# Offset convolution: summing columns of taps on VectorE before shifting them on TensorE

## The chip, the cores and the metric

One core of one Trainium2 chip. The metric is the device time of one execution in microseconds (us), a median of several. The profile is one execution of each kernel; PE is TensorE's matmuls, PEld its weight loads, DVE VectorE, ACT ScalarE, POOL GpSimd, and SPq the queue from which SyncE (SP) issues transfers.

## The reference, cut to what matters

Two layers on an image batch of shape (2, 256, 128, 128) in fp32. The first holds three deformable branches with dilations 1, 9 and 12. Each needs its sampling offsets first: 18 numbers per pixel, from a 3x3 convolution of the normalised image.

```python
def _branch(x, w_off, w_def, lw, lb, pad, dil):
    off = _conv(x, w_off, pad, dil)            # 18 channels out, 3x3, dilated: the part changed
    y = _deform_dw(x, off, w_def, pad, dil)    # bilinear sampling at the offsets
    return gelu(_ln2d(y, lw, lb))
x1 = _branch(x, off_w1, def_w1, bw1, bb1, 1, 1)
x2 = _branch(x, off_w2, def_w2, bw2, bb2, 9, 9)
x3 = _branch(x, off_w3, def_w3, bw3, bb3, 12, 12)
# ... a 1x1 convolution, norms and an MLP, then a second layer: group norm and a ternary 3x3 convolution
```

## The kernel before

It runs in three stages: the offsets and, from them, "hat" functions (the bilinear weights, stored to memory); the sampling; the final convolution. The change is in the first stage, which does image 0 and then image 1. Per row, TensorE multiplies 128 pixels by all 27 x 18 tap weights and the result goes into a ring of 40 rows (`zr`). Then, for 8 rows at a time (a group, `G`; 16 groups per image), each of the 27 taps is taken from the ring with its row offset and shifted along the image by a product with a 0/1 matrix.

```python
def columns(g):                                   # 4 rows of the image: a column step
    xt = pool.tile([P, KC, R, W], F32, name="xa", tag="xa", bufs=4)
    nc.scalar.dma_start(xt, x[b]...)              # the image's load, ScalarE's queue
    # ... normalise, transpose, store the rows to `table` (SyncE's queue)
    for r in range(R):
        # pz = xt[row r] @ wz, two products
        (nc.scalar.copy if r % 2 else nc.vector.tensor_copy)(zr[:, (g * R + r) % ZRING, :], pz[:, 0:NZ])

def offsets(G):
    todo = []                                     # (branch, tap, shift, row, ring slot, rows)
    for br, dil in enumerate(DILS):
        for tap in (4, 0, 1, 2, 3, 5, 6, 7, 8):
            # ... cut where the ring wraps, or where the image ends
    for i, (br, tap, dx, r0, s, n) in enumerate(todo):
        z0 = (br * 9 + tap) * 18
        nc.tensor.matmul(pov[:, r0:r0+n, br*18:br*18+18], lhsT=k["shift"][:, dx, :],
                         rhs=zr[:, s:s+n, z0:z0+18], start=i == 0, stop=i == len(todo) - 1)
    # offs <- po; offs is stored (SyncE) and split into bf16 parts

def make_hats(g, parts, r0):                      # twice per group
    # ... transposes of the parts (pp), then six blocks:
    for h0 in range(0, 9 * NH, HCH):
        # ph = two products; hb = |ph| by ScalarE (bufs=8); hb = min(hb, 1) - 1 by VectorE
        # store_hats: 4 or 6 stores of 18 to 144 KB per block, all nc.sync.dma_start
```

All stores and the 1 MB loads for the normalisation's statistics (`xt`) leave through SyncE's one queue, in program order. A group of 8 rows is 56 hat stores, two table stores and one offset store: 59 issues.

## Time and profile before

8689.66 us median of 3 runs (8687.26 to 8691.22).

| what | before |
|---|---|
| span of the profiled run | 8672.1 us |
| first stage, to the last hat store | 0 to 1281 us |
| PE busy over the span, DVE busy | 90%, 69% |
| records of offset products (two per fp32 product) | 1872 |
| mean granted TensorE clock | 0.952 |

Read it by stages. The first stage is only 15% of the time; a share of the whole span says nothing about it. The prediction shows the lines. The lines are as the profile gives them.

### The profile page before, as it was taken

The page shows a single profiled execution, that of the slowest core. Times are in us where ns is not written, and L with a number is a line of the kernel's source. Part 1 is how long each engine was busy: PE and PEld are TensorE (multiplying, and loading weights), DVE is VectorE, ACT ScalarE, POOL GpSimd, SP SyncE. Part 2 cuts the span into 40 slices and gives each one's busy share as a digit, 9 for nine tenths or more (in the row PEclk, how much of TensorE's full clock was granted, in tenths as well). Part 3 has the DMA queues.
Part 4 walks back from the last instruction along what each step waited for, and adds up shares of the span by engine and source line. Part 5 has one row for each costly group of instructions (what it writes and reads, how often), then busy time and mean ns, then how long its engine had stood idle before and what let it go on. Part 6 is the DMA issues. An engine that isn't in the chain of part 4 may idle for free. (4 is left out here: it accounts for less than half of the span.)

```text
span 8672.1 us, 125470 instructions
## 1 busy us (share of the span) xinstructions
PE 7799.2 (90%) x41584; PEld 5835.1 (67%) x41584; DVE 5965.6 (69%) x13113; ACT 4513.1 (52%) x9542; POOL 718.1 (8%) x1292
## 2 busy tenths in 40 slices
PE   6977967898999999999979999989999979999999
PEld 3644637777787778777777787777877744444444
DVE  5434436889898998987688989898988843222222
ACT  1332324566666666666656666666666752221221
POOL 0000000011111111111101111111111110000000
PEclk9988978999999999999999999999999989999999
DMA  7445448999999999987799899999898821111111
GB/s 239 138 144 165 139 138 224 245 243 241 248 241 248 243 245 244 242 240 218 190 244 244 244 244 243 245 243 248 239 247 238 237 99 56 57 56 54 58 57 41
DMA packets 994675, 1661.78 MB, mean 192 GB/s; under 512 B 139424, under 2 KB 540112, under 8 KB 989656
## 3 DMA queue, kind: packets, MB, share of 16 engines
q1 hardware_dynamic: 976600, 1620.03, 68.3%
q10 hardware_dynamic: 17408, 33.56, 1.3%
q8 instruction: 333, 5.46, 0.3%
q14 instruction: 334, 2.74, 0.1%
HBM read 1385.08 MB, written 268.09 MB: 191 GB/s over the span
## 5 line engine op out<-in xcount | busy, mean ns | idle before, releaser
L766 PE MATMUL pm<-A,xs 128*128 128x180 f32 (+2 forms) x22288 | 3661.4, 321 | 569.6 <-ACT ev L775 530.9
L766 PEld LDWEIGHTS pm<-A,xs 128*128 128x128 f32 x22288 | 3456.9, 197 | 776.5 <-ACT ev L775 630.8
L775 ACT COPY ev<-pm 128x360 f32<-128x360 f32 (+2 forms) x5572 | 2285.6, 455 | 1528.6 <-DVE ring L740 749.8
L740 DVE SCALAR_TENSOR_TENSOR ring<-ev,defw,ring 128x256 f32<-128x256 f32 (+5 forms) x6272 | 2787.3, 464 | 211.3 <-ACT ev L775 42.0
L1078 PE MATMUL pc<-cring,signs 128*128 128x512 bf16 x6912 | 1503.5, 380 | 4.1 <-ACT cring L1059 3.4
L696 DVE TENSOR_TENSOR A<-hy,hx 128x768 f32<-128x768 f32 x1130 | 1017.9, 947 | 343.2 <-DMA hx<-hats 177.8
L1078 PEld LDWEIGHTS <-signs 128*128 128x128 bf16 x6912 | 671.8, 97 | 835.4 <-issue 8.4
L481 ACT ACTIVATE T<-T,rs 128x256 f32<-128x256 f32 x1280 | 663.6, 595 | 4.0 <-POOL rs L477 3.9
L1090 DVE SCALAR_TENSOR_TENSOR o<-pc,wpn,o 128x512 f32<-128x512 f32 x128 | 96.1, 751 | 675.1 <-PE pc L1078 675.0
L474 POOL TENSOR_SCALAR rs<-mv 128x4 f32<-128x4 f32 x320 | 113.0, 353 | 5150.6 <-DVE mv L472 4290.9
L440 PE MATMUL hp<-T,w 128*128 128x512 f32 x1024 | 489.0, 602 | 7.8 <-ACT T L559 7.8
L1086 ACT ACTIVATE o<-xl,l1b 128x512 f32<-128x512 f32 x128 | 92.2, 722 | 739.4 <-DMA out_x<-o 715.7
L207 PE MATMUL pz<-wz,xa 128*128 128x486 f32 x1024 | 469.2, 583 | 6.6 <-DVE zr L214 3.5
L470 DVE BATCH_NORM_STATS2 st<-T 128x6 f32<-128x256 f32 x1280 | 447.4, 413 | 22.5 <-ACT T L462 22.4
L440 PE MATMUL h<-hT,w 128*128 128x512 f32 x1024 | 460.1, 592 | 0.0
L1059 ACT CAST cring<-rest 128x768 bf16<-128x768 f32 (+1 forms) x256 | 211.8, 828 | 462.7 <-PE pc L1078 296.9
L493 PEld LDWEIGHTS zc<-ident,T 128*128 128x128 f32 x2560 | 339.6, 155 | 98.7 <-issue 61.4
L287 ACT ACTIVATE hb<-ph 108x512 f32<-108x512 f32 x384 | 222.6, 598 | 338.8 <-DMA hats<-hb 229.8
L509 ACT ACTIVATE T<-zc,bb,bw 128x512 f32<-128x512 f32 x384 | 278.6, 780 | 227.6 <-PE zc L493 226.9
L493 PE MATMUL zc<-ident,T 128*128 128x128 f32 x2560 | 379.2, 294 | 19.2 <-ACT T L481 13.8
L476 POOL TENSOR_TENSOR rs<-rs,mhalf 128x4 f32<-128x4 f32 x320 | 368.5, 1152 | 0.0
L462 ACT COPY T<-tp 128x512 f32<-128x512 f32 x640 | 344.2, 597 | 36.4 <-PE tp L460 35.3
(107 smaller groups left out, 5381.2 us busy)
## 6 DMA issues: line engine op xcount, KB each, us to landing
hy<-hats SPq DMA_DIRECT2D x1114, 384.0 KB
hx<-hats SPq DMA_DIRECT2D x1114, 384.0 KB
xs<-table SPq DMA_DIRECT2D x1876, 128.0 KB
g12d<-T SPq DMA_DIRECT2D x128, 512.0 KB
other<-g12d SPq DMA_DIRECT2D x128, 512.0 KB
xl<-x1d SPq DMA_DIRECT2D x120, 384.0 KB
hats<-hb SPq DMA_DIRECT2D x256, 144.0 KB
xa<-in_x ACTq DMA_DIRECT2D x64, 512.0 KB
```

Source lines behind the costliest of these rows:

```text
L207: nc.tensor.matmul(pz[:, 0:NZ], lhsT=xt[:, c, r, :], rhs=k["wz"][:, c, :], start=c == 0, stop=c == KC - 1,)
L440: nc.tensor.matmul(out, lhsT=w, rhs=v, start=i == 0, stop=i == n - 1)
L462: nc.scalar.copy(Tv[:, 2 * h : 2 * h + 2, :].rearrange("p j c -> p (j c)"), tp)
L470: pin(nc.vector.bn_stats(st[:, j, :], Tv[:, j, :]))
L476: nc.gpsimd.tensor_tensor(rs[:, 0, :], rs[:, 0, :], mhalf[:, 0:NB4], ALU.pow)
L481: nc.scalar.activation(Tv[:, j, :], Tv[:, j, :], AF.Identity, scale=rs[:, 0, j : j + 1], bias=rs[:, 1, j : j + 1],)
L493: nc.tensor.transpose(zc[:, j * P : (j + 1) * P], Tv[:, j, c * P : (c + 1) * P], ident)
L696: nc.vector.tensor_tensor(dst, hy[:, :, i0 * W : i1 * W].rearrange("p t (i w) -> p t i w", w=W), hx[:, :, i0 * W : i1 * W].rearrange("p t ...
L740: nc.vector.scalar_tensor_tensor(dst, src, w, dst, ALU.mult, ALU.add)
L766: nc.tensor.matmul(pm[:, j, 0:n], lhsT=xts[b, Rt][T + j][:, c * P : (c + 1) * P], rhs=A[:, m0:m1, AO + (T + j) * CI : AO + (T + j + 1) * C ...
L775: nc.scalar.copy(ev[:, m0:m1, T * CI : (T + 2) * CI].rearrange("p m (t j) -> p t m j", j=CI), pm[:, :, 0:n].rearrange("p t (m j) -> p t m ...
L1078: nc.tensor.matmul(pc, lhsT=signs[:, k, ky * 3 + kx, m * P : (m + 1) * P], rhs=xc[:, i, k, ky : ky + R, kx : kx + W], start=j == 0, stop=j ...
```

## The change

Shifting along the image (x) is the same for the three taps of a column (same kx, three ky). So VectorE first adds the three rows of the ring that belong to one output row, for all three kx at once, and TensorE shifts the sums: 9 products per group, with no cuts, in place of 27 and more.

```diff
+            zs = pool.tile([P, 3, ZG, 3 * 18], F32, name="zs", tag="zs", bufs=2)
             for br, dil in enumerate(DILS):
-                for tap in (4, 0, 1, 2, 3, 5, 6, 7, 8):
-                    ...
+                for y, n, mid in rows(0, y0, y1):
+                    for ya, na, up in rows(-1, y, y + n):
+                        nc.vector.tensor_tensor(zs[...], mid[...], up, ALU.add)
+                    # ... plain copies where a row has no neighbour above
+                for y, n, down in rows(1, y0, y1):
+                    nc.vector.tensor_tensor(dst, dst, down, ALU.add)
-            for i, (br, tap, dx, r0, s, n) in enumerate(todo):
-                nc.tensor.matmul(... rhs=zr[:, s : s + n, z0 : z0 + 18] ...)
+            for br, dil in enumerate(DILS):
+                for kx in range(3):
+                    nc.tensor.matmul(
+                        pov[:, :, br * 18 : br * 18 + 18],
+                        lhsT=k["shift"][:, k["dxs"].index((kx - 1) * dil), :],
+                        rhs=zs[:, br, :, kx * 18 : kx * 18 + 18],
+                        start=br == 0 and kx == 0, stop=br == 2 and kx == 2)
```

(cut: the boundaries of the image and of the ring)

More of the change, by code (lines that the diff above doesn't have):

```diff
@@ L221, in offsets, with rows @@
             pov = po[:, 0 : ZG * NOFF].rearrange("p (r n) -> p r n", n=NOFF)
-            todo = []
+            zs = pool.tile([P, 3, ZG, 3 * 18], F32, name="zs", tag="zs", bufs=2)
             for br, dil in enumerate(DILS):
-                for tap in (4, 0, 1, 2, 3, 5, 6, 7, 8):
-                    ky, kx = tap // 3 - 1, tap % 3 - 1
-                    y = max(G * ZG, -ky * dil)
-                    y1 = min((G + 1) * ZG, H - ky * dil)
+                def rows(ky, y, y1):
+                    y, y1 = max(y, -ky * dil), min(y1, H - ky * dil)
                     while y < y1:
@@ L230, in offsets @@
                         n = min(y1 - y, ZRING - s)
-                        todo.append((br, tap, k["dxs"].index(kx * dil), y - G * ZG, s, n))
+                        z0 = (br * 3 + ky + 1) * 54
+                        yield y, n, zr[:, s : s + n, z0 : z0 + 54]
                         y += n
-            for i, (br, tap, dx, r0, s, n) in enumerate(todo):
-                z0 = (br * 9 + tap) * 18
-                nc.tensor.matmul(
-                    pov[:, r0 : r0 + n, br * 18 : br * 18 + 18],
-                    lhsT=k["shift"][:, dx, :],
-                    rhs=zr[:, s : s + n, z0 : z0 + 18],
-                    start=i == 0,
-                    stop=i == len(todo) - 1,
-                )
+                y0, y1 = G * ZG, (G + 1) * ZG
+                for y, n, mid in rows(0, y0, y1):
+                    done = y
+                    for ya, na, up in rows(-1, y, y + n):
+                        if ya > done:
+                            nc.vector.tensor_copy(
+                                zs[:, br, done - y0 : ya - y0], mid[:, done - y : ya - y]
+                            )
+                        nc.vector.tensor_tensor(
+                            zs[:, br, ya - y0 : ya - y0 + na], mid[:, ya - y : ya - y + na], up,
+                            ALU.add,
+                        )
+                        done = ya + na
+                    if done < y + n:
+                        nc.vector.tensor_copy(
+                            zs[:, br, done - y0 : y + n - y0], mid[:, done - y : n]
+                        )
+                for y, n, down in rows(1, y0, y1):
+                    dst = zs[:, br, y - y0 : y - y0 + n]
+                    nc.vector.tensor_tensor(dst, dst, down, ALU.add)
[5 more added lines that the diff above has]
+                        rhs=zs[:, br, :, kx * 18 : kx * 18 + 18],
+                        start=br == 0 and kx == 0,
+                        stop=br == 2 and kx == 2,
+                    )
             offs = pool.tile([P, ZG, NOFF], F32, name="offs", tag="offs", bufs=2)
```

## The prediction

> **What bounds the kernel now.** I read the page's slices first, because a change in one stage is worth only what that stage can give back. The span of 8672.1 us has three stages. The offset convolution lives in the first one, which ends at about 1281 us (slices 1 to 6 of 216.8 us each); then come the sampling (to about 7100 us) and the final convolution.
>
> ```profile
> PE   6977967898999999999979999989999979999999
> DVE  5434436889898998987688989898988843222222
> ...
> PEclk9988978999999999999999999999999989999999
> ```
>
> The first stage handles the two images one after the other, and each time TensorE (PE) is nearly full and then falls away. So I cut the stage at the points where the last row of column products has been copied out (573 us for image 0, 1148 us for image 1) and at the ends of the images' stores:
>
> ```profile
> core 0: us, PE busy (x) PEld busy (x) DVE busy (x) ACT busy (x) POOL busy (x), PEclk, DMA share, GB/s
> 139.00:573.00 434.00, 417.76 (x2014) 268.48 (x2013) 181.99 (x399) 139.55 (x256) 0.00 (x0) 0.97 0.50 144
> 573.00:675.00 102.00, 47.98 (x147) 23.42 (x146) 23.43 (x57) 24.36 (x41) 0.00 (x0) 0.55 0.44 125
> 752.00:1148.00 396.00, 390.58 (x1879) 249.06 (x1878) 164.66 (x363) 126.65 (x233) 0.00 (x0) 1.00 0.49 141
> 1148.00:1281.00 133.00, 74.99 (x294) 42.55 (x292) 36.44 (x88) 37.51 (x65) 0.65 (x1) 0.61 0.45 127
> ```
>
> Two regimes per image: a body of 434 and 396 us with PE busy 96 and 99% and VectorE (DVE) only 42%, and a tail of 102 and 133 us in which no engine is half full. The waits of PE in the body of image 1 confirm that nothing holds it there: 5.4 us in all.
>
> ```profile
> PE ph L279 <- ACT hb L287: 3.6, 4, 1.1
> PE pz L207 <- DVE xa L154: 1.1, 2, 0.7
> PE tpa L193 <- ACT ts L198: 0.7, 3, 0.2
> ```
>
> In the tail I looked for what is full, and it is the queue of SyncE (SP), which issues the small stores of the hat functions one by one:
>
> ```profile
> 656.96 0.36 SPq L308 DMA_DIRECT2D hats<-hb  x1
> 657.37 0.49 SPq L304 DMA_DIRECT2D hats<-hb  x1
> 657.90 0.37 SPq L308 DMA_DIRECT2D hats<-hb  x1
> 658.37 0.34 SPq L304 DMA_DIRECT2D hats<-hb  x1
> 658.75 0.38 SPq L308 DMA_DIRECT2D hats<-hb  x1
> 659.17 0.78 SPq L304 DMA_DIRECT2D hats<-hb  x2
> ```
>
> Each start follows the one before by about 0.42 us. Counted over 600 to 675 us there are 169 issues in 75 us, 0.444 us each. An image has 16 groups of 8 rows, each with 56 such stores, and 48 other stores: 944 issues, some 415 us at that rate. So SP is a second, hidden limit close behind PE: in the body it is occupied only 71% (635 issues at 0.427 us in 380 us), in the tail it sets the pace at 26 to 28 us a group. Last, what the offset products cost:
>
> ```profile
> L235 PE MATMUL po<-zr,shift 128*128 128x144 f32 x606 | 84.9, 287 | 0.0
> L207 PE MATMUL pz<-wz,xa 128*128 128x486 f32 x429 | 195.9, 576 | 1.1 <-DVE xa L154 1.1
> L260 DVE TENSOR_TENSOR rest<-offs,parts 128x432 f32<-128x432 f32 x13 | 7.9, 606 | 0.3
> 305.32 3.39 PE L235 MATMUL po<-zr,shift 128*128 128x18 f32 x28
> 308.99 2.29 PE L235 MATMUL po<-zr,shift 128*128 128x72 f32 x18
> ```
>
> The mean of 287 ns is a latency; the matmuls overlap. The runs give the real price: 3.39 us for 28, 2.29 us for 18, and over all runs of 4 or more in the body 113.6 us for 856, 0.133 us a record.
>
> **What the Trainium skill says.** "TensorE: Matmul & The Clock Gate", Back-to-back issue gap: the spacing of a stream of weight loads and matmuls is set by both together, about 81 ns at 128 columns. The trace agrees in kind, not in size: fp32 offset records come 0.121 to 0.136 us apart, nearly whatever their width (the slivers left by the ring's wrap cost as much as whole blocks), so the count of products is what counts. "VectorE: DVE Perf Modes", The TRN2 errata: an fp32 tensor_tensor takes (N+151)/0.96 ns; for N=432 that is 607 ns, and the trace has 606 to 607 ns for L260. "Perfetto Trace Analysis", DMA Instruction — HWDGE: a DMA instruction's time in the profile is the issuing sequencer's and the descriptor generator's, not the movement of the data. That fits: stores of 18 and 36 KB all take about 0.37 us of SP while the DMA share is 0.44. The same page, Optimization Strategy: the most contended engine can change between regimes; here it does, twice per image.
>
> **The change part by part.** Removed: the trace has 1872 records of offset products; the program has 936, so an fp32 product is two records. After the change there are 9 per group, 288 products, 576 records. That is 1296 fewer, times 0.133 = 172 us of PE, 86 us per image. Not all lies on the path. In the bodies of the built order the changed program still has about 252 records per image, against 858 and 786 in the trace, so about 606 and 534 go: 80 and 71 us. Before the first group's first store another 18 products (36 records) per image go: 5 us each, most of it given back below. What is left falls in the tails, where PE idles half of the time and nothing is gained.
>
> Added: the built program has 226 additions and copies for the column sums, where the ring does not wrap six additions of 432 elements per group. At 607 ns for a full one, and N/0.96 plus the fixed 157 ns for the cut ones, they come to 118 us of DVE, 3.7 us per group. DVE goes from about 13.6 us of 33 per group (42%) to 17.3 of some 28.5 (61%): it does not become the bound. They lie beside PE's work, except that the first products of a group now wait for an eviction and one addition (0.66 + 0.61 us) where no other column's work stands between; in the order of PE the nine products of a group are mostly surrounded by others. For the first group of each image nothing stands in between: 1 to 3 us back.
>
> Moved: in the SP order the stores stay in their sequence of 56 per group, two table stores and one of the offsets between. PE's order still ends the columns with twelve groups of hats done and four to go. So the tail stays: four groups at SP's pace, 102 and 133 us.
>
> PE per group now, from the pitches: 32 column records at 0.405 us (13 us), 24 hat records at 0.295 (7.1), 16 plane transposes at 0.165 (2.7), 16 table transposes at 0.13 (2.1), 58.5 offset records at 0.133 (7.8): 32.7 us, and the traced spacing of the stores' groups is 34.5 us in image 0 and 33.8 us in image 1. After: 18 offset records, 2.4 us, sum 27.3 us. SP needs 59 issues at 0.44, 26 us. Two stages in tandem with 27.3 and 26 us and only eight hat buffers between them (two thirds of a group's twelve), and with only two buffers for the table's rows, which leave through the same SP queue: I choose 29 us a group, 1.7 us of stalls over PE's own need (the traced spacing now exceeds PE's need by 1.1 to 1.8 us, while SP has 29% to spare). Gain of the bodies: 12 x (34.5 - 29) + 12 x (33.8 - 29) = 66 + 58 = 124 us. The starts give about nothing net, the tails, the sampling and the end nothing. 8690 - 124 = 8566, rounded to 8565 us.
>
> **The rivals.** (1) PE's saving comes through whole: SP keeps up without stalls. Gain 80 + 71 + a few, about 155 us, 8535 us. For it: PE's order spreads the hat products evenly, and SP's 26 us are below 27.3. Against it: SP's queue is in order and arrives in bursts of 56, and the hats already waited for stores in the body of image 1 (ACT 50.8 us in 33 waits), when SP was far from full. (2) SP takes over as the bound and PE stalls behind it: 31 us a group, gain 76 us, 8614 us. For it: just those waits; a late store holds ACT, then DVE behind its hb steps, then the additions queued behind those, and then the products. Against it: the offsets of a group are made two groups before its hats are stored, so the additions have slack. (3) The additions make DVE late: each group pays 1 to 3 us where PE waits for the last sum, gain 60 to 100 us. DVE at 61% in program order speaks for some of it. (4) Nothing gained, since the stores end the stage anyway. Against: SP was idle for 29% of the body because PE fed it no faster, so an earlier hat is an earlier store.
>
> **Range and chances.** 8565 us, 8525 to 8620 us. The low end is rival 1 and a little more, the high end rival 2. Faster by over 2% means under about 8516 us, a gain of 174 us, as much as all PE time removed, tails included: 0.06. Slower by over 2% would need 174 us lost in a stage where nothing grows but an engine at 61%: 0.01. Within 2%: 0.93.
>
> **What would show it.** Right: 576 offset records of about 0.13 us pitch; some 226 new VectorE instructions of 118 us in all; the groups of stores 28 to 30 us apart in the bodies; SP occupied over 80% there; tails still some 100 to 130 us at the 0.50 clock; the stage ends near 1157 us and the later stages take as long as before. PE waits for hb and DMA grow in the body. It would be wrong if the groups came at 33 us still (the additions are on the path, shown by PE waiting at the offset products), if the tails grew by what the bodies lost (SP the only bound), or if the later stages changed because buffers or order moved there.

## The result, and the profile after

The changed kernel takes 8624.71 us (8612.09 to 8632.42, 4 runs) against 8688.46 us of the kernel before on the same chip (8682.11 to 8691.22): 64 us less, where 124 were predicted, and 5 us above the stated range. The ratio is 0.9926, with a 95% interval of 0.9909 to 0.9943; a ratio here is the mean time of one kernel's runs over that of the other's runs of the same rounds, so it isn't quite the quotient of the medians. Executions over 1.5% slower than the fastest of the same kernel are left out of the means. The result is correct.

First the parts that I had counted. Offset products and additions in the profile of the changed kernel, grouped by shape; the columns are count, then busy us and mean ns of one:

```profile
L258 PE MATMUL po<-zs,shift 128*128 128x144 f32 x576 | 90.0, 295 | 19.4 <-DVE offs L266 19.4
L244 DVE TENSOR_TENSOR zs<-zr 128x432 f32<-128x432 f32 x72 | 40.9, 601 | 11.0 <-ACT zr L214 11.0
L255 DVE TENSOR_TENSOR zs<-zs,zr 128x432 f32<-128x432 f32 x68 | 40.0, 600 | 32.1 <-ACT zr L214 31.9
```

576 records, as computed, and 0.6 us for a full addition. The durations of all 226 new VectorE instructions sum to 117 us. So the counts of what was removed and added are as predicted; what it was worth is not.

The two images again, with the right cuts: from about the first hat store to the last copy into the ring (the body), and from there to the last hat store (the tail). Busy us of each engine in each stretch, kernel before:

```profile
145.00:534.00 389.00, 382.45 (x1850) 245.43 (x1850) 165.74 (x364) 124.64 (x230) 0.00 (x0) 1.00 0.49 142
535.00:675.00 140.00, 76.71 (x292) 43.64 (x291) 36.91 (x86) 37.45 (x65) 0.00 (x0) 0.60 0.47 133
757.00:1149.00 392.00, 386.25 (x1860) 246.84 (x1860) 161.86 (x357) 125.74 (x232) 0.00 (x0) 1.00 0.49 141
1149.00:1281.00 132.00, 74.32 (x292) 42.43 (x291) 36.44 (x88) 37.22 (x65) 0.65 (x1) 0.61 0.44 126
```

and the changed kernel:

```profile
131.00:495.00 364.00, 335.93 (x1292) 182.61 (x1290) 207.50 (x460) 124.53 (x230) 0.00 (x0) 0.96 0.54 152
495.00:636.00 141.00, 73.36 (x230) 35.82 (x229) 40.10 (x93) 38.33 (x66) 0.00 (x0) 0.56 0.49 138
723.00:1082.00 359.00, 330.51 (x1291) 181.57 (x1289) 200.34 (x447) 125.18 (x230) 0.00 (x0) 0.97 0.53 150
1082.00:1222.00 140.00, 69.46 (x231) 33.34 (x230) 39.61 (x95) 38.38 (x66) 0.65 (x1) 0.59 0.47 130
```

The bodies shrink from 389 to 364 and from 392 to 359 us. PE was 98% busy in them and is now 92%, at a granted clock that falls from 1.00 to 0.96 and 0.97: TensorE is still the fullest engine, but something now holds it up. How much of the loss is the lower clock, no run isolates. DVE rises from 42% to 56 and 57% and is far from full. The sum of the whole stage, from the exact starts of the stores: first store 14.4 us earlier, bodies 25.6 and 32.1 us shorter, tails 1.1 and 7.2 us longer, the stretch between the images 4 us longer: 60 us. The later stages differ by 2 us.

What PE waits for in the body of image 1 (us in total, times, longest), changed kernel; before it was 5.4 us in three rows:

```profile
PE ph L302 <- ACT hb L310: 9.0, 16, 1.6
PE pz L207 <- DVE xa L154: 7.1, 5, 2.0
PE po L258 <- DVE offs L266: 6.1, 4, 2.4
PE tpa L193 <- ACT ts L198: 5.6, 9, 2.0
PE pp L294 <- DVE parts L284: 0.5, 1, 0.5
```

28.3 us, from four different sides, and hardly any of it at the sums `zs`. I read waits scattered like this as back pressure from further on: the hat blocks (`hb`), the offsets (`offs`) and the table rows (`ts`) are all buffers that come free when a store has landed. So I took SyncE's queue apart. Over the first 11 groups of 56 hat stores, counted from single records (a line of the timeline can merge several stores and hide a wait between them):

| body | us per group | SP issuing | gaps under 0.15 us | longer waits of SP |
|---|---|---|---|---|
| before, image 0 / 1 | 35.1 / 35.3 | 24.1 / 23.9 | 3.2 / 3.2 | 7.7 / 8.1 |
| after, image 0 / 1 | 33.0 / 32.8 | 23.8 / 23.7 | 3.2 / 3.2 | 6.0 / 5.9 |

The queue's own work is 27 us a group, the same in both kernels, and equal to what TensorE needs after the change (27.3 us by the prediction). What the change took away is about 2 us a group of SP's waiting, and 6 us of waiting stayed. A stretch of that queue in the changed kernel (start us, us):

```profile
302.75 0.94 SPq L199 DMA_DIRECT2D table<-ts  x2
303.74 0.79 SPq L275 DMA_DIRECT2D offd<-offs  x1
304.62 1.31 SPq L331 DMA_DIRECT2D hats<-hb  x1
305.99 0.83 SPq L327 DMA_DIRECT2D hats<-hb  x1
306.87 0.73 SPq L331 DMA_DIRECT2D hats<-hb  x1
307.65 0.78 SPq L327 DMA_DIRECT2D hats<-hb  x2
308.47 0.36 SPq L331 DMA_DIRECT2D hats<-hb  x1
310.17 0.29 SPq L327 DMA_DIRECT2D hats<-hb  x1
```

Most hat stores take 0.36 to 0.39 us as before, but the three that follow the table's and the offsets' stores take 1.31, 0.83 and 0.73 us, and between 308.83 and 310.17 us the queue waits.

### The profile page after: what moved, and what is told of

The parts are those of the page before. It is cut to its first block, busy times and chain, and to the rows that moved or that the text cites.

```text
span 8610.4 us, 123172 instructions
## 1 busy us (share of the span) xinstructions
PE 7669.1 (89%) x40288; PEld 5674.0 (66%) x40288; DVE 6061.3 (70%) x13339; ACT 4516.2 (52%) x9542; POOL 718.7 (8%) x1292
```

## The experiments

Two theories at first. A: the path of the hat stores through SyncE's queue sets the pace. B: VectorE is late because of the additions. C was a variant: VectorE held up by the offsets' buffers. Chips differ by some 10 us, so each run is told against the kernel before on the same chip; the change alone gained 64 us by that measure. The interval of a gain is about 14 us to each side, so two gains that differ by less than some 20 us are not told apart. The last column is the time from an image's first hat store to its last, divided by 16 groups, in the profiled run.

| run | us | before, same chip | gain | ratio, 95% interval | us per group, image 0 / 1 |
|---|---|---|---|---|---|
| before | | 8688 | | | 33.1 / 32.7 |
| the change | 8625 | 8688 | 64 | 0.9909 to 0.9943 | 31.6 / 31.2 |
| e1 no additions | 8632 | 8681 | 49 | 0.9932 to 0.9966 | 31.8 / 31.3 |
| e2 changed, two queues | 8382 | 8681 | 298 | 0.9639 to 0.9672 | 25.8 / 25.3 |
| e3 before, two queues | 8505 | 8681 | 176 | 0.9784 to 0.9817 | 28.4 / 28.1 |
| e4 four offset buffers | 8636 | 8681 | 44 | 0.9938 to 0.9971 | 32.0 / 31.6 |
| e5 ten hat buffers | 8633 | 8677 | 44 | 0.9934 to 0.9967 | 31.6 / 31.4 |
| e6 other stores moved | 8558 | 8677 | 119 | 0.9853 to 0.9886 | 29.7 / 29.1 |
| e7 one block in six | 8623 | 8677 | 55 | 0.9918 to 0.9951 | 31.9 / 30.2 |
| e8 no additions, two queues | 8389 | 8677 | 288 | 0.9658 to 0.9695 | 26.0 / 25.7 |
| e9 changed, loads moved | 8590 | 8677 | 88 | 0.9890 to 0.9923 | 30.5 / 30.5 |
| e10 before, loads moved | 8656 | 8677 | 21 | 0.9962 to 0.9995 | 32.4 / 32.7 |
| e11 one in six and loads | 8584 | 8679 | 95 | 0.9876 to 0.9909 | 30.8 / 30.7 |
| e12 hats alone on SP | 8553 | 8679 | 126 | 0.9841 to 0.9874 | 29.0 / 29.1 |
| e13 one block in three | 8461 | 8676 | 215 | 0.9733 to 0.9765 | 27.2 / 26.2 |
| e14 statistics loads moved | 8578 | 8676 | 98 | 0.9876 to 0.9909 | images overlap, see there |

**e1: no additions.** Wrong result; the additions and `zs` are gone, the rest is the changed kernel.

```diff
-                        rhs=zs[:, br, :, kx * 18 : kx * 18 + 18],
+                        rhs=zr[:, G*ZG % ZRING : G*ZG % ZRING + ZG, (br*3+1)*54 + kx*18 : (br*3+1)*54 + kx*18 + 18],
```

> A wrong result on purpose: the nine products per group read the middle row of the column products directly, with no additions by VectorE; everything else is the changed kernel. Theory A (the hat stores in SyncE's one queue, with the few buffers behind them, set the pace of about 31 us a group): within 15 us of the changed kernel's 8625, groups still 30 to 32 us apart in the bodies. Theory B (VectorE in program order is late because of the 118 us of additions): down by 60 to 100 us to about 8525 to 8565, groups 27 to 28 us apart. Theory C (VectorE is held by the offsets' two buffers, whose stores stand behind the hat stores in the queue): little change, 0 to 20 us.

8631.6 us, a gain of 49 us in place of 64, groups at 31.8 and 31.3 us. With 117 us of VectorE's work removed, nothing is gained. Theory B falls.

**e2 and e3: two queues.** Every second of the six hat blocks is stored from GpSimd's queue, in the changed kernel (e2) and in the kernel before (e3).

```diff
-                    store_hats(g, q, h, hb[p : p + m])
+                    store_hats(g, q, h, hb[p : p + m], nc.gpsimd if h0 // HCH % 2 else nc.sync)
```

> The changed kernel with every second block of hats stored from GpSimd's queue instead of SyncE's. Theory A: groups at PE's own need, 27 to 28 us in the bodies, and tails of about 60 us in place of about 140: down by some 150 us to 8450 to 8500. Theory B: the tails shorten but the bodies stay at 31 us: 8540 to 8580. Theory C: between them, since the offsets' stores stand behind half as many others.

> The kernel before with the same two queues. Theory A: TensorE still sets about 33 us a group in its bodies, only the tails shorten: 8590 to 8630, so that the change is worth 110 to 150 us once the stores are out of the way, against 64 with one queue. Theory B: the difference between the two kernels stays about 64 us.

8382.47 and 8505.27 us, both correct, both better than expected. The change, which was worth 64 us with one queue, is worth 123 us here, which happens to be near what I had predicted. The bodies of e2, same columns as above:

```profile
137.00:497.00 360.00, 339.90 (x1402) 191.06 (x1401) 247.22 (x535) 145.59 (x269) 212.56 (x371) 0.99 0.79 220
577.00:933.00 356.00, 338.72 (x1408) 190.86 (x1408) 223.37 (x491) 145.85 (x271) 216.56 (x377) 1.00 0.66 182
```

As long as in the changed kernel, but with 13.5 groups of hats stored in each in place of 11.0, so a group takes 26 to 27 us in the body, about TensorE's own need. The tails fall from 140 to about 50 us. And image 1's first copy into the ring comes at 524 us, while the hats of image 0 are stored until 549; with one queue its statistics loads stand behind those stores, and that copy came at 677 us. In the built program the loads stand between the groups of image 0 now. So e2 changes two things besides the queues: the start of image 1, which e13 and e14 take apart, and the order of TensorE's work, which no run isolates: see the end of the next section.

**e4: four buffers for the offsets.**

```diff
-            offs = pool.tile([P, ZG, NOFF], F32, name="offs", tag="offs", bufs=2)
+            offs = pool.tile([P, ZG, NOFF], F32, name="offs", tag="offs", bufs=4)
-        hatw = ap.tile([P, 2, 9 * NH], F32, name="hatw32")
+        hatw = k["zr"]...[:, 0 : 18 * NH]          # staged in the ring, to make room
```

> The changed kernel with four buffers for the offsets in place of two (room made by staging the hat matrix in the ring). Theory C: VectorE's 65 us of waits for the offsets' store go and 30 to 60 us of time with them, 8565 to 8595. Theory A: VectorE waits elsewhere instead, within 15 us of 8625. Theory B: within 15 us.

8636.45 us, no gain over the change. Removing VectorE's waits for the offsets' store does not help; theory C falls too.

**e5: ten hat buffers** (`bufs=8` to `bufs=10` at `hb`, with the same room made).

> The changed kernel with ten buffers for the blocks of hats in place of eight (the hat matrix staged in the ring, as in the run with four offset buffers, to make room). Theory A1 (the number of instructions that SyncE's queue has to issue sets the pace; deeper buffers only lengthen the queue): within 15 us of 8625 to 8636. Theory A2 (the eight buffers, each held until its stores have landed, set the pace): a quarter more of them takes 40 us or more off, 8590 or less.

8632.85 us, no gain over the change: two more hat buffers do not help either.

**e6: the table's and the offsets' stores from GpSimd's queue.**

```diff
-            nc.sync.dma_start(tv[2 * REACH + g * R : ...], ts)
+            nc.gpsimd.dma_start(tv[2 * REACH + g * R : ...], ts)
-            nc.sync.dma_start(offd[b][G * ZG : ...], offs)
+            nc.gpsimd.dma_start(offd[b][G * ZG : ...], offs)
```

> The changed kernel with the table's and the offsets' stores (3 of the 59 issues of a group) on GpSimd's queue, all hats still on SyncE's. Theory A1: 56 instead of 59 issues, 30 us instead of 31.5 us a group: 20 to 50 us less, 8575 to 8605. Theory A3 (the order in one queue binds: a table or offset store at its head waits, and the hats behind it with it): the waits of SyncE in the body, 4 to 5 us a group, go with them, 8520 or less.

8557.9 us: 55 us more gained than by the change alone. That is between the two expectations: more than three issues in 59 explain, less than all of SP's waits. SP's longer waits in the body did not fall (7.4 and 6.9 us a group), but TensorE's waits there fell from 28 to 7 and 6 us, so its columns end at 459 us. Fewer groups are stored by then: the tails, 5 groups of 28 us after the change alone, are 6 groups of 25 us here.

**e7: one block in six from GpSimd's queue** (`nc.gpsimd if h0 // HCH == 2`).

> The changed kernel with one of the six blocks of hats of each half group stored from GpSimd's queue: SyncE issues 51 instead of 59 per group. Theory A1: the spacing falls with the count, 31.5 x 51 / 59 = 27.2 us, which is TensorE's own need, and the tails by an eighth: some 100 to 120 us less, 8505 to 8525. Theory A2 or A3: the buffers, or the stores at the head of the queue, still bind: 8570 to 8610.

8622.59 us: no gain over the change, though SP issues 51 times per group in place of 59. Its issuing falls to 21 us a group in the body, and its longer waits rise to 10.5 and 9.3. So the count of issues alone isn't the cause; this was my clearest miss among the experiments.

**e8: no additions, two queues** (e1 and e2 together, wrong result).

> A wrong result on purpose: two queues as in the best run so far (8382 us), and no additions by VectorE. If the additions lie beside TensorE's work even where TensorE sets the pace: within 15 us of 8382. If they delay the products once the stores no longer bind: 30 to 60 us less, 8320 to 8350.

8389.37 us, no faster than e2. The additions lie beside TensorE's work even where TensorE sets the pace.

**e9 and e10: the image's loads from GpSimd's queue**, in the changed kernel and in the kernel before. In the built program the stores of SyncE and these loads of ScalarE take turns in eight completion semaphores, and the profile puts most of SP's waits down to them. In the body of image 1, before:

```profile
SPq L304 <- DMA xa<-in_x: 54.1, 11, 9.2
SPq L308 <- DMA xa<-in_x: 21.4, 10, 6.9
```

and after the change:

```profile
SPq L327 <- DMA xa<-in_x: 25.0, 12, 6.4
SPq L331 <- DMA xa<-in_x: 22.1, 11, 5.4
```

```diff
-            nc.scalar.dma_start(xt, x[b]...)
+            nc.gpsimd.dma_start(xt, x[b]...)
```

> The changed kernel with the image's loads (64 in all, 512 KB each) issued from GpSimd's queue instead of ScalarE's; all 59 stores of a group stay on SyncE. In the built program the stores and these loads share eight completion semaphores in turn, so that a hat store waits for the load that had its semaphore before, and a load for a store. Theory L (this tie is what holds the stores back: the waits of SyncE for the image's loads, 53 us in the first image): those waits vanish, groups at 27 to 28 us, 60 to 160 us less than the changed kernel's 8625, 8465 to 8565. Theory A1 (the plain issue rate of 59 stores): at most 20 us less, 8605 or more.

> The kernel before with the same loads moved to GpSimd's queue. Theory L: TensorE still needs 32.7 us a group, the stores keep up, only the tails and the last groups of the bodies gain: 20 to 70 us below 8680, 8610 to 8660, so that the change is worth 100 us or more in this pair. Theory A1: within 15 us of 8680, and the change is worth about 60 us again.

8589.85 and 8656.06 us. The waits for the loads are gone, but most of SP's longer waits stay (4.5 and 5.1 us a group in e9, 6.0 and 5.9 before): the profile now puts them down to hat blocks that aren't made yet and to other stores. Both kernels gain about the same, 24 us and 21 us, and the change is worth 66 us in this pair. The tie costs some 20 us; it isn't what took the change's gain.

**e11 and e12: combinations.** e7 with e9; and e6 with e9, so that only hats are left to SP in the bodies.

> The changed kernel with both edits at once: one block of hats in six stored from GpSimd's queue (51 instead of 59 issues of SyncE per group; alone it gained nothing) and the image's loads on GpSimd's queue too (alone it gained 35 us). If the issues of SyncE count as soon as its waits for the loads are gone: 51 issues are 23.4 us by the traced 0.46 a piece, and the 3 us of waits that stay make 26 to 28 us a group, TensorE's own need: 8480 to 8530. If the count of issues never mattered and only the tie did: 8580 to 8600, as with the loads alone.

> The changed kernel with nothing but hat stores in SyncE's queue during the two bodies: the table's stores, the offsets' stores and the image's loads all on GpSimd's. If the two gains found alone (67 us for the stores, 35 us for the loads) come from different waits they add: 8510 to 8535. If they are the same wait: 8550 to 8565. Either way the tails stay at about 25 us a group, because a group is still 56 issues of SyncE.

8583.97 and 8553.2 us. e11 gains no more than e9: 51 issues do as badly as 59, even without the loads' tie. e12 is within 7 us of e6, no clear difference: the two waits are largely the same time. A group takes 29 us from first store to last, the best that one queue did for all the hats. The bodies of e12, same columns as above:

```profile
149.00:468.00 319.00, 312.18 (x1273) 177.46 (x1272) 198.39 (x439) 117.60 (x223) 52.63 (x64) 0.99 0.62 179
696.00:1015.00 319.00, 311.69 (x1283) 177.32 (x1283) 194.65 (x431) 118.98 (x227) 50.98 (x62) 1.00 0.61 175
```

They are 40 to 45 us shorter than after the change alone, with TensorE 98% busy and waiting only 6 and 7 us, and in the body of image 0 SP's waits are mostly for hats not yet made (57 of 72 us). So here the queue does not hold TensorE up in the bodies. What an image still loses against e2 lies in the tails: TensorE ran its columns up to 5.6 groups ahead of the hats, only 10 groups are stored when they end, and the 6 left go at SP's pace of 25 us.

**e13 and e14: what is the body's, what is image 1's early start.** e13 stores two blocks in six from GpSimd's queue (`h0 // HCH % 3 == 2`; 39 issues of SP per group), with image 1's statistics loads still behind image 0's hats. e14 is the changed kernel with those loads on GpSimd's queue and all stores on SP.

> The changed kernel with two of the six blocks of hats of each half group (20 of 56 stores) on GpSimd's queue; SyncE issues 39 per group. In its built order TensorE does two column steps per group of hats from the start, as in the run with half the stores moved, but image 1's statistics loads still stand behind image 0's hats in SyncE's queue. If the store path is what binds: bodies at TensorE's 27 us a group and tails near 55 us, the early start of image 1 missing: 8430 to 8480. If moving a part does as little as one block in six did: 8580 to 8620.

> The changed kernel with the loads for the statistics (32 of 1 MB) on GpSimd's queue, all stores on SyncE's. This takes away only image 1's wait behind image 0's hats. The bodies should stay at 32 us a group and the tails at about 140 us; image 1's columns start up to 60 us earlier or more, under image 0's tail: 8530 to 8590. If SyncE's stores are the whole limit, the columns of image 1 only pile up behind the hats, and the stage ends as soon as 32 groups have been stored: 30 us or less gained, 8595 or more.

8460.69 us is in the range for a limit in the store path. 8578.0 us is in the first of e14's ranges; by its gain over the change on the same measure, 34 us, it can't be told from the second, in which SyncE's stores are the whole limit. e13 gains 151 us more than the change alone, with groups at 27.2 and 26.2 us from first store to last and tails of 70 and 63 us. e2 adds 83 us to that: in the profiles its stretch between the images is 53 us shorter, and its tails, with 31 issues a group in place of 39, are 33 us shorter together. In e14 the early start comes (image 1's columns begin at 606 us, before image 0's hats are through), and it gains only those 34 us: the first store came at 170.2 us, later than before, the last at 1189.1, so 32 groups in 1018.9 us, 31.8 us each. Filling the gap between the images doesn't quicken the stores.

**The version that beats both kernels** is e2: 8382.47 us, correct, 0.9656 of the kernel before (0.9639 to 0.9672).

## Why the prediction was wrong, point by point

**The count of products: right; their price: somewhat too high.** 576 records, 0.137 us each where all 18 of a group come in one run (2.47 us in the median). But from e3 to e2, where the stores hold TensorE up least, 556 fewer records take 61 and 62 us off its busy time in the two bodies, 0.11 us a record in place of 0.133, and the bodies are only 47 and 45 us shorter: TensorE waits 20 and 17 us in e2, 6 and none in e3. So the 155 us of rival 1 were not reached even there.

**The additions: right.** 226 instructions, 117 us (118 predicted), and e1 and e8 show that they cost nothing in time, with one queue or two. Rival 3 is ruled out.

**The tails and the later stages: right in kind.** The tails stayed (140 and 132 us before, 141 and 140 after). My cut at 573 us was wrong, and so were twelve groups in the body and four in the tail: 11.0 to 11.1 groups are stored by the end of the columns in both kernels, about 5 are left.

**The step that failed:** "I choose 29 us a group, 1.7 us of stalls over PE's own need". In the bodies a group took 33.0 and 32.8 us, only 2.1 and 2.5 us less than before, where I had forecast 5.5 and 4.8 less; the bodies gave 58 us together in place of 124. I had seen both limits, 27.3 us for TensorE and 26 for SP, and named their coupling, but took SP's waits in the body for idleness that would go as soon as TensorE fed it faster. Two sizes were off. SP's work is 27 us a group in the body, since stores that follow the offsets' store take longer; and 6 us of its waits stayed. That makes 33 us, 4 more than I chose, and TensorE, which waited 5 to 6 us in a body before, waited 28. Why those waits stayed is not settled (see below). Rival 2, "SP takes over as the bound and PE stalls behind it", was the nearest: its gain of 76 us was 12 us too high. That is in part luck, since it assumed 31 us a group in the bodies, where 33 was measured, and an issuing rate alone does not explain the waits (e7).

**Where the gain went.** With the hats split over two queues the same change is worth 123 us, close to the 124 of the prediction. That closeness is luck: the bodies give 92 of it in the profiles, and the rest is mainly a shorter stretch between the images (27 us) and an earlier first store (12 us). TensorE, 94 and 95% busy, paces the bodies there at 26 to 27 us a group. So a good part of the gain was lost on the side of the hat stores: e2, e3 and e13 show that taking stores off SP brings it back, and e1 and e8 that the additions don't matter. They don't show that SP's issuing as such is the bound, since the built order changed with the queues.

**What stays open.** How the loss divides between SP's queue and the order of TensorE's work. The additions, two more pairs of buffers (e4, e5), the loads' semaphores (24 us, and 21 in the kernel before) and the other stores (55 us) have been tried one at a time; none is it alone, and 51 issues were no better than 59 while 39 were 151 us better. The order changed with this, and no run isolates it: with 59 or 51 issues TensorE runs the columns ahead, to 4 groups beyond the hats, and has done the products of 11.5 to 11.8 groups of hats when the columns end; with 39 or 31 it keeps them 2.9 groups ahead throughout, and has done 13.8. The order is fixed when the program is built. The traces show how it can cost time by itself: the more groups are left for the tail, the more run at SP's pace alone while TensorE is half idle, and in e12 this is what remains. An estimate from e12 and e13: a body of 360 us with 13.5 groups and 2.5 groups more at 25 us make about 423 us an image, where e12 took 464. A kernel with one queue and the order of e13 would tell; I did not build it.

## What to carry to other kernels

When an engine is near 100% busy, work out what each queue behind it needs per unit of work, with its waits as the trace has them, before counting a saving on that engine: here the next limit stood level with the new need, and a good part of the gain was lost. Look also at the order in which the built program does the work: it decides how much is left for a stretch in which the queue alone sets the pace. Here the loss showed as small waits in many places; adding buffers one by one gained nothing, and splitting the stores over two queues gained 234 us more than the change by itself. For the case that descriptor generation binds, the Trainium skill suggests in "Perfetto Trace Analysis", DMA Optimizations, to balance the transfers over the engines that can issue them; e2 and e13 did so and gained 298 and 215 us, though no run shows that descriptor generation was what bound.

## What the Trainium skill lacked or had wrong

- "DMA: Bandwidth & Descriptors", Issuing engines are not separate DMA queues, says that issuing from several engines only saves the sequencer's time to initiate a transfer, which is usually small beside the transfer. The trace has no landing times to compare with, but the sum was not small here: 896 hat stores per image cost SP 0.37 us each in the median and 0.40 on average, and SP issues for 24 of the 33 us of a group, at a DMA share of 0.53 in the body. Storing half of them from GpSimd's queue gained 176 us in the kernel before and 298 us together with the change (the built order changed too). The advice of "Perfetto Trace Analysis", DMA Optimizations, fits better, and the two pages should refer to each other.
- No page found says that stores issued just after another can take longer on SP: after an offsets' store the next three hat stores took 1.30, 0.87 and 0.73 us in the median of 32 groups, in place of 0.37. Why is not shown.
- "TensorE: Matmul & The Clock Gate", Back-to-back issue gap, gives 81 ns at 128 columns. An fp32 product is two records here, each 0.121 to 0.137 us (a run's length over its records) at 18 to 144 columns; the section has no row for fp32.
- "VectorE: DVE Perf Modes", The TRN2 errata: its formula, which gives 607 ns for an fp32 addition of 432 elements, holds to about 1% also where the inputs are 54-element pieces of longer rows (600 to 601 ns).
